# A four-layer graph network: layer 0 by stationary weights, layer 1 begun in layer 0's end, layer 2's tables between layer 1's last lists

## The chip, the cores and the metric

The kernel runs on one core of a Trainium2 chip. The metric is device time in microseconds (us) of one execution. A core has a matrix engine (TensorE, PE in the profile, with its weight loads as PEld), a vector engine (VectorE, DVE), a scalar engine with function tables (ScalarE, ACT), a general engine that here also issues all indirect transfers (GpSimd, POOL), and SyncE (SP), which issues direct transfers. SBUF is the on-chip memory, PSUM holds TensorE's sums.

## The reference

Input x has 8 batches of 2048 nodes with 64 features; adj is a 2048 × 2048 graph of some 8 edges a node, its own edge included. Four layers follow each other; each is `x = layernorm(x + layer(x))`:

```python
# layer 0: graph attention with scores s1(i) + s2(j)
h = layernorm(matmul(x * node_weights + x, W))
e = leaky_relu(h @ a1 [i] + h @ a2 [j], 0.2)
out = elu(softmax(where(adj, e, -big)) @ h + h)
# layer 1: a softmax over the neighbours for each feature
feat = softplus(x * w0 / sqrt(2) + b0)
attn = softmax(where(adj, feat * wa + ba, -big), over neighbours)
out = sum over neighbours of attn * feat
# layer 2: mean over the neighbours, two products, relu twice, layernorm
out = layernorm(relu(x @ W_self + mean(x[neighbours]) @ W_neigh + biases))
# layer 3: attention with scores <h_i, h_j>, four heads, then an output head of the same kind, layernorm
```

## The kernel before, in words

All of x stays in SBUF as `X`, 16 tiles of 128 nodes (NT = 16), each node with 8 × 64 values. A layer that sums over neighbours does so in one of two ways.

*By list.* A tile's neighbours are found by ten indirect gathers (`gather`, L203–204, on POOL): each brings 128 rows of a table in DRAM. There are five slots (GS = 5) for each of two groups of 64 nodes (NG = 2). They are used in three steps per tile, `TOGETHER = ((0, 3), (1, 4), (2,))`, so with 4, 4 and 2 gathers; the code calls a step a quad. A selection matrix `Sel` (0 or 1, fp8) in blocks of 32 nodes adds the gathered rows into their nodes by a matmul.

*By matrix.* For the tiles 0 to DENSE − 1 the adjacency itself stands in SBUF as `ET` in fp8. A block of 128 × 128 is multiplied with the rows of a whole tile, and these rows are split into three bf16 pieces (high, middle, low), whose three matmuls add up to f32.

The stages, in the order of time:

1. The adjacency is read, lists, `Sel` and `ET` are made; the table of layer 0 (`htab0`, 512 values a row) is written.
2. **Layer 0** (L432–524), all 16 tiles by list, in an order written by hand (`manual_schedule`). In each round of the loop: `fetch` gathers the next tile's ten blocks into `hs` (two buffers of a whole tile); `weights` forms the scores and two exponentials; `divide` and `combine` end an earlier tile; `weigh` multiplies every gathered row by its weight on DVE (L476, five products of 128 × 1024) and adds the products up with `self_`, the selection in f32, as stationary operand (L482), and the denominators with 12 small matmuls (L484); `activate` does the ELU and, every second tile, the layer norm's statistics; `normalise` applies them on ACT (L170, eight activations a tile). The score of the neighbour, a2·h, stands in the place of the first feature of a row; `combine` gets that feature back as minus the sum of the others (L498), since h is centred.
3. **Layer 1's rows** (`make_rows`, L570–597), four tiles at once, in an order left to the scheduler: exp and log on ACT (softplus), logits on DVE, exp on ACT, a product on DVE (L590), a write to the table `rtab`; then the pieces into `R`: high on POOL (L593), rest on DVE (L595), middle on ACT (L596), low on POOL (L597). TensorE adds the first three dense tiles' matmuls behind (L605).
4. **Layer 1's sums.** `finish` divides (L614) and adds to X, and where both tiles of a pair are done, normalises them. The dense tiles 3 to 7 run in steps of one block, and between them the quads of tiles 15 down to 8 (L660); gathers go two quads ahead into 8 buffers.
5. **Layer 2's tables** (L812–824). For every tile: X turned by TensorE, two products into `py` (two buffers), `y` copied and written to `ytab` by SyncE, `Y`'s pieces by POOL (high, L818), DVE (rest, L822), ACT (middle, L823), POOL (low, L824), and `S` by DVE (L819). Again the scheduler sets the order.
6. **Layer 2's sums**, by hand: dense steps (L982), quads (L962), and in their gaps each tile's chain of normalisations. `show` copies a finished tile on POOL into `Xo` and writes it to layer 3's table `xtab` (L908–912).
7. **Layer 3**, by hand, with two further lists of 160 gathers each.

In stages 2, 4, 6 and 7 POOL issues gathers in program order; a gather waits until its buffer is free, and what stands behind it on POOL waits too. SyncE's queue works in order as well.

Of the kernel before, what the change touches and what calls it, by code (L numbers as in the profile page):

```python
# [48 lines left out]
def kernel(ctx: ExitStack, tc: tile.TileContext, ins: dict, out: bass.AP):  # L49
# [150 lines left out]
    DENSE = 8  # L200
# [23 lines left out]
    htab0 = dram.tile([N + 1, BD], F32, name="htab0")  # L224
    no_row(htab0)
    l0 = ExitStack()
    wp = l0.enter_context(tc.tile_pool(name="l0w", bufs=1))
    H = wp.tile([P, NT, BD], F32, name="H")
# [33 lines left out]
    for k, a in enumerate((a1, a2)):  # L262
# [5 lines left out]
        if k:  # L268
            first_col = wp.tile([P, 2], F32, name="first_col")
            nc.vector.tensor_copy(first_col, Wv[:, :, 0])  # L270
            nc.vector.tensor_copy(Wv[:, :, 0], Wa[:, 1])
            nc.vector.tensor_copy(Wa[:, 1], first_col)

# [13 lines left out]
    def node_products(t0, wk, ps):  # L287
# [4 lines left out]
        for q in range(HALF):  # L292
# [14 lines left out]
            nc.vector.tensor_reduce(var[:, q], sq[:, :, 1:], AX.X, ALU.add)  # L307
            held.append(ph)
        v4, r4, t4 = (a.rearrange("p q (a k) -> p q a k", k=2) for a in (var, rstd, tmp))
        nc.vector.tensor_tensor(t4, pq[:, :, :, 1], pq[:, :, :, 1], ALU.mult)  # L310
        nc.vector.tensor_tensor(var, var, tmp, ALU.add)
        nc.vector.scalar_tensor_tensor(var, var, 1.0 / D, eps.unsqueeze(2).to_broadcast(var.shape), op0=ALU.mult, op1=ALU.add)
        inv_sqrt(*(a.rearrange("p q b -> p (q b)") for a in (rstd, var, tmp)))
        for q, ph in enumerate(held):
            t = t0 + q
            nc.vector.tensor_tensor(H[:, t].rearrange("p (b d) -> p b d", d=D),
                                    ph.rearrange("p a (k d) -> p (a k) d", d=D), along(rstd[:, q]), ALU.mult)
            nc.sync.dma_start(htab0[t * P:(t + 1) * P, :], H[:, t])
# [116 lines left out]
    wk = l0.enter_context(tc.tile_pool(name="l0k", bufs=2))  # L435
    ps_e = l0.enter_context(tc.tile_pool(name="l0pse", bufs=2, space=PSUM))
    ps_o = l0.enter_context(tc.tile_pool(name="l0pso", bufs=3, space=PSUM))
    ps_w = l0.enter_context(tc.tile_pool(name="l0psw", bufs=1, space=PSUM))
    held, zs, stats = {}, {}, {}

    def fetch(it):
        hs = wk.tile([P, GS * NG, B, D], F32, name="hs")
        for s in range(GS):
            for g in range(NG):
                gather(hs[:, s * NG + g].rearrange("p b d -> p (b d)"), htab0, it, s, g)
        selTf = wk.tile([P, GE], F32, name="selTf")
        nc.scalar.activation(selTf, SelT[:, it], AF.Copy)
        self_ = wk.tile([P, NG, NQ, GB], F32, name="self_")
        nc.scalar.activation(self_, Sel[:, it], AF.Copy)
# [3 lines left out]
        pe = ps_e.tile([P, GS, NG * B], F32, name="pe")  # L453
        for s in range(GS):
            nc.tensor.matmul(pe[:, s], selTf[:, s * P:(s + 1) * P], s1g.rearrange("p g b -> p (g b)"), start=True, stop=True)
        held[it] = hs, self_, pe

    def weights(it):
        hs, self_, pe = held[it]
        wm = wk.tile([P, GS * NG, B], F32, name="wm")  # L460
        nc.vector.tensor_tensor(wm, pe.rearrange("p s (g b) -> p (s g) b", b=B), hs[:, :, :, 0], ALU.add)
        w = ps_w.tile([P, GS * NG, B], F32, name="w")
        nc.vector.scalar_tensor_tensor(w, wm, 0.2, wm, op0=ALU.mult, op1=ALU.max)
        nc.scalar.activation(wm, w, AF.Exp)
        nc.scalar.activation(w, w, AF.Exp)  # L465
        held[it] = hs, self_, w, wm

    def weigh(it):
        hs, self_, w, wm = held[it]
        po = ps_o.tile([P, BD], F32, name="po")  # L470
        pd = ps_w.tile([P, B], F32, name="pd")
        for n, ss in enumerate(TOGETHER):
            for s in ss:
# [11 lines left out]
        held[it] = po, pd  # L485

    def divide(it):
        po, pd = held.pop(it)
        rd = wk.tile([P, B], F32, name="rd")
        nc.vector.reciprocal(rd, pd)  # L490
        z = zs[it] = po.rearrange("p (b d) -> p b d", d=D)
# [1637 lines left out]
```

## Time and profile before

| | us |
|---|---|
| three runs: median (lowest to highest) | 1773.65 (1766.21 to 1776.88) |
| profiled execution: its time, its span | 1766.28, 1764.5 |
| adjacency, tables of layer 0 | 0 to 184 |
| layer 0, gathers | 184 to 397 |
| layer 0, end | 397 to 445 |
| layer 1, rows | 445 to 529 |
| layer 1, sums | 529 to 684 |
| layer 2, tables | 684 to 748 |
| layer 2, sums | 748 to 924 |
| layer 3 | 924 to 1764 |

Over the span TensorE is busy 1388.2 us (79%), DVE 1197.8 (68%), ACT 931.5 (53%), POOL 870.1 (49%). The bounds of the stages are those between the first and last instructions of a kind, rounded. A line of groups reads: line, engine, operation, target and sources, their shapes, how often; busy time and mean ns of one; idle time of the engine before them, and what ended most of it. A line of the timeline begins with the start and the duration in us, and the idle time before it stands in brackets.

### The profile page before, as it was taken

What the parts mean: (1) busy time and instruction counts of PE and PEld (TensorE: products, weight loads), DVE (VectorE), ACT (ScalarE), POOL (GpSimd) and SP (SyncE); (2) the same over time, 40 slices, a digit from 0 to 9 for tenths busy, and PEclk for the clock granted to TensorE, in tenths of its full rate; (3) what the DMA queues carried; (4) which work ended last, traced back from release to release, by engine and by line L of the source; (5) the groups of instructions that cost most, each with busy time, mean ns of one, the idle gap of its engine ahead of it and who ended that gap; (6) DMA issues with size and microseconds to landing.
All of it is one profiled execution on the core that took longest, in us unless ns stands there. A gap on an engine that the chain in (4) does not pass through costs nothing.

```text
span 1764.5 us, 38665 instructions
## 1 busy us (share of the span) xinstructions
PE 1388.2 (79%) x15230; PEld 953.8 (54%) x15264; DVE 1197.8 (68%) x2931; ACT 931.5 (53%) x1943; POOL 870.1 (49%) x820
## 2 busy tenths in 40 slices
PE   4673454651689996898839999999999986999994
PEld 3673232330233333632217877777777774878783
DVE  5989389996666564755764666666666654787787
ACT  5763244555942132534654655656655543577674
POOL 0000677670665551766526455454554515777761
PEclk9655567666799998999968999999999998999997
DMA  6550566660227982256614555555555526787771
GB/s 185 182 173 26 174 196 199 190 200 10 95 96 242 332 313 86 90 169 189 174 43 126 144 144 149 150 148 138 150 153 143 144 77 205 206 233 219 212 214 45
DMA packets 154135, 280.64 MB, mean 159 GB/s; under 512 B 64892, under 2 KB 91452, under 8 KB 151868
## 3 DMA queue, kind: packets, MB, share of 16 engines
q0 software_dynamic: 56320, 189.44, 35.8%
q1 hardware_dynamic: 80986, 84.45, 16.5%
q10 hardware_dynamic: 16640, 4.20, 1.1%
q8 instruction: 123, 2.02, 0.5%
q14 instruction: 66, 0.54, 0.1%
HBM read 237.60 MB, written 40.42 MB: 158 GB/s over the span
## 4 chain that ended last, share of the span: by engine, by line
PE 42%; DVE 13%; ACT 6%; issue 5%; POOL 3%; DMA 1%; DVEq 0%; SPq 0%; ACTq 0%; POOLq 0%
PE pscore L1081 8%; PE pa L605 6%; PE po L1103 5%; PE pt L1068 4%; PE pscore L1044 4%; PE pa L660 2%; PE ps L1385 2%; PE po L1424 2%; PE py L812 2%; DVE z L1156 2%; POOL hs L204 1%; PE pt L1362 1%; PE pa L982 1%; ACT z L849 1%; PE pscore L1166 1%
## 5 line engine op out<-in xcount | busy, mean ns | idle before, releaser
L204 POOL DMA_INDIRECT hs<-htab,src x160 | 153.2, 958 | 238.6 <-issue 221.5
L204 POOL DMA_INDIRECT xs<-xtab,src x160 | 205.9, 1287 | 115.6 <-PE po L1103 63.3
L1087 DVE SCALAR_TENSOR_TENSOR w<-w,Sel 128x640 f32<-128x640 f32 (+2 forms) x160 | 153.2, 958 | 135.3 <-ACT w L1084 134.6
L605 PE MATMUL pa<-R,ET 128*128 128x512 bf16 x746 | 178.3, 393 | 52.0 <-POOL R L593 35.3
L204 POOL DMA_INDIRECT hs<-ktab,src x160 | 158.7, 992 | 63.6 <-issue 35.7
L1081 PE MATMUL pscore<-U,xsT 64*128 64x80 f32 (+2 forms) x2560 | 183.0, 283 | 0.0
L1081 PEld LDWEIGHTS pscore<-U,xsT 64*128 64x128 f32 x2560 | 157.7, 190 | 43.5 <-ACT xsT L1070 22.7
L605 PEld LDWEIGHTS <-ET 128*128 128x128 fp8e4 x768 | 75.2, 100 | 163.6 <-issue 84.4
L170 ACT ACTIVATE X<-X,ln_m,ln_r 128x64 f32<-128x64 f32 x256 | 87.2, 427 | 138.7 <-DVE ln_m L162 138.7
L1070 ACT COPY xsT<-pt 128x512 f32<-128x512 f32 x160 | 93.6, 585 | 104.1 <-PE pt L1068 104.1
L1084 ACT ACTIVATE w<-pscore 128x640 f32<-128x640 f32 (+2 forms) x160 | 119.5, 747 | 47.1 <-PE pscore L1081 45.2
L1103 PE MATMUL po<-w,xs 128*64 128x88 f32 (+2 forms) x3072 | 139.0, 236 | 0.7 <-DVE w L1087 0.7
L1068 PE MATMUL pt<-ident,xs 128*128 128x128 f32 x640 | 106.8, 290 | 23.5 <-DMA xs<-xtab,src 22.8
L1103 PEld LDWEIGHTS po<-w,xs 128*64 128x64 f32 x3072 | 113.4, 137 | 14.9 <-DVE w L1087 0.8
L204 POOL DMA_INDIRECT rs<-rtab,src x80 | 75.9, 949 | 62.4 <-PE pa L660 42.6
L614 DVE RECIPROCAL rec<-pa 128x256 f32<-128x256 f32 x32 | 54.1, 1729 | 64.0 <-PE pa L660 38.0
L1385 PE MATMUL ps<-U,hsT 128*128 128x64 f32 x768 | 93.8, 269 | 1.5 <-ACT hsT L1363 1.5
L476 DVE TENSOR_TENSOR hs<-hs,w 128x1024 f32<-128x1024 f32 x80 | 91.8, 1213 | 2.7 <-ACT w L465 2.6
L1385 PEld LDWEIGHTS ps<-U,hsT 128*128 128x128 f32 x768 | 92.5, 192 | 1.9 <-ACT hsT L1363 1.7
L982 PE MATMUL pa<-Y,ET 128*128 128x512 bf16 x372 | 89.1, 386 | 3.1 <-DVE rest L822 2.1
L1472 ACT ACTIVATE z<-z,ln_m,ln_r 128x64 f32<-128x64 f32 x240 | 83.5, 431 | 14.1 <-DVE ln_m L1460 14.1
L204 POOL DMA_INDIRECT rs<-ytab,src x80 | 76.8, 960 | 26.8 <-issue 17.0
(636 smaller groups left out, 3059.8 us busy)
## 6 DMA issues: line engine op xcount, KB each, us to landing
at<-in_adj SPq DMA_DIRECT2D x16, 1024.0 KB
R<-itab SPq DMA_DIRECT2D x60, 256.0 KB
rtab<-r SPq DMA_DIRECT2D x16, 512.0 KB
ptab<-hp SPq DMA_DIRECT2D x16, 384.0 KB
hi<-ptab SPq DMA_DIRECT2D x16, 384.0 KB
ktab<-hb SPq DMA_DIRECT2D x16, 260.0 KB
X<-in_x ACTq DMA_DIRECT2D x16, 256.0 KB
htab<-H SPq DMA_DIRECT2D x16, 256.0 KB
```

Source lines behind the costliest of these rows:

```text
L170: nc.scalar.activation(v[:, b], v[:, b], AF.Identity, scale=rstd[:, k:k + 1], bias=nmr[:, k:k + 1])
L204: nc.gpsimd.indirect_dma_start(out=dst, out_offset=None, in_=table[:, :], in_offset=bass.IndirectOffsetOnAxis(ap=src[:, it, s, g:g + 1], a ...
L476: nc.vector.tensor_tensor(wx, wx, along(w[:, own].rearrange("p g b -> p (g b)")), ALU.mult)
L605: nc.tensor.matmul(po[h].rearrange("p a f -> p (a f)"), ET[:, jt, it * P:(it + 1) * P], R[:, jt, q, h].rearrange("p a f -> p (a f)"), star ...
L982: nc.tensor.matmul(sums[it], ET[:, jt, it * P:(it + 1) * P], Y[:, jt, q].rearrange("p a n -> p (a n)"), start=(jt == 0 and q == 0), stop=( ...
L1068: nc.tensor.transpose(pt[:, p], xss[k][:, p * P:(p + 1) * P], ident)
L1070: nc.scalar.copy(xsTs[k], pt)
L1081: nc.tensor.matmul(pscore[:, k_, f0:f0 + HN * ni].rearrange("p (h i) -> p h i", i=ni), xsT[half, p], Us[it][half, p, :, i0:i0 + ni], start ...
L1084: nc.scalar.activation(w.rearrange("p k a h i -> p k (a h i)"), pscore[:, :, 0:NP * HN * ni], AF.Exp)
L1087: nc.vector.scalar_tensor_tensor(wt, wt, 3.0e38, edge, op0=ALU.min, op1=ALU.mult)
L1103: nc.tensor.matmul(po[half, p, :, a - blk * GB:b - blk * GB], xs[:, f0:f0 + D], w[:, k_, p, :, a - WINDOWS[s][0]:b - WINDOWS[s][0]], start ...
L1385: nc.tensor.matmul(pscore[:, g, 2 * p:2 * p + 2], hsT[:, g, p], U[:, p, :, node_block(g, k)], start=False, stop=(p == NP - 1))
```

## The change

DENSE becomes 7, so that tile 7 too goes by list in layers 1 and 2: 9 tiles, 27 quads, 90 gathers in each of the two.

Layer 0: a row of `htab0` gets 66 values a batch: the score, a one, and the 64 features. The weights are multiplied into the selection (`W`, four DVE products a tile), and `W` is the stationary operand against the gathered rows (32 columns against 65 values, 96 matmuls a tile); the column of ones gives the denominator. `hs` is held in half tiles with five buffers.

Layer 1's rows move into layer 0's loop: `normalise` also does the exp, `soften` the log every second round, then `logits` and `row_out`, which writes `rtab`. What is left of layer 0's end and of the rows is written out by hand. The pieces are no longer made from the row in SBUF: `load_rows` reads it back from `rtab` on SyncE into `rf` (two buffers), and `pieces` splits it, for tiles 0 to 4 (SOON = 5) on POOL alone, in the end of layer 0, for the others on ACT and DVE between the matmuls. Tile 0's first five blocks are multiplied in the end of layer 0.

Layer 1's sums run in an order by hand: 18 of the 27 quads (AMID) between the dense steps, six gathers in flight (8 buffers before), a finished tile's statistics and scaling some steps later (`later`, `due`). Layer 2's tables (`turn_x`, `products`) are made between the last nine quads, with `py` in one buffer. Buffers in these parts are waited for tile by tile (`reuse_waits="tile"`), and `S` and `Y` are one tile for each of the 16. The code of layer 2's sums and of layer 3 changes in names only.

The core of the diff:

```diff
-    DENSE = 8
+    DENSE = 7
...
     def fetch(it):
-        hs = wk.tile([P, GS * NG, B, D], F32, name="hs")
...
+        hs = [wk.tile([P, GS, B, E0], F32, name="hs", bufs=5) for _ in range(NG)]
...
     def weigh(it):
-                nc.vector.tensor_tensor(wx, wx, along(w[:, own].rearrange("p g b -> p (g b)")), ALU.mult)
...
+                nc.vector.tensor_tensor(W[:, of[0]:of[-1] + 1], Sel[:, it, g, of[0]:of[-1] + 1].unsqueeze(2).to_broadcast(shape),
+                                        pe[:, 1, g, ss[0]:ss[-1] + 1].unsqueeze(3).to_broadcast(shape), ALU.mult)
+            for n in range(NQ // 2):
+                for t in range(B):
+                    j, b = divmod(t, HB)
+                    for q in (n, n + NQ // 2):
+                        s, k = QS[q]
+                        nc.tensor.matmul(pv[node_block(g, k), j, b], W[:, q, t], hs[g][:, s, t, 1:], start=(n == 0 and b == 0),
+                                         stop=(n == NQ // 2 - 1 and b == HB - 1))
...
+            if k >= 3:
+                normalise(k - 3)
+                if k % 2 == 0:
+                    soften(k - 4)
+            if k % 2 and k >= 5:
+                logits(k - 5)
+                logits(k - 4)
+            if k % 2 == 0 and k >= 6:
+                row_out(k - 6)
+                row_out(k - 5)
...
+    def load_rows(jt):
+        if jt < NT:
+            rfs[jt] = ra.tile([P, 2 * BD], F32, name="rf", bufs=2)
+            nc.sync.dma_start(rfs[jt], rtab[jt * P:(jt + 1) * P, :])
+
+    def pieces(jt):
+        if jt < NT:
+            rf = rfs.pop(jt)
+            hi, mid, lo = (R[jt][:, q].rearrange("p h a n -> p (h a n)") for q in range(3))
+            if jt < SOON:
+                nc.gpsimd.tensor_copy(hi, rf)
+                nc.gpsimd.tensor_tensor(rf, rf, hi, ALU.subtract)
+                nc.gpsimd.tensor_copy(mid, rf)
+                nc.gpsimd.tensor_tensor(lo, rf, mid, ALU.subtract)
+                return
+            nc.scalar.copy(hi, rf)
+            nc.vector.tensor_tensor(rf, rf, hi, ALU.subtract)
+            nc.scalar.copy(mid, rf)
+            nc.vector.tensor_tensor(lo, rf, mid, ALU.subtract)
...
+        load_rows(0)
+        load_rows(1)
+        row_out(NT - 6)
+        row_out(NT - 5)
+        for t in range(SOON):
+            pieces(t)
+            load_rows(t + 2)
+            add_rows(0, t)
+        combine(NT - 2)
+        divide(NT - 1)
+        activate(NT - 2)
+        normalise(NT - 3)
+        soften(NT - 4)
+        combine(NT - 1)
+        activate(NT - 1)
+        logits(NT - 4)
+        logits(NT - 3)
+        normalise(NT - 2)
+        normalise(NT - 1)
+        row_out(NT - 4)
+        row_out(NT - 3)
+        soften(NT - 2)
+        for t in (NT - 2, NT - 1):
+            logits(t)
+        for t in (NT - 2, NT - 1):
+            row_out(t)
...
+    AMID, LATE = 18, 14
+    n = 0
+    with tc.manual_schedule(engines=engines):
+        fetch(IN_FLIGHT)
+        pieces(SOON)
+        load_rows(SOON + 2)
...
+        for k, (it, jt) in enumerate(steps):
+            if made < NT and (k % 3 == 2 or jt + 2 >= made):
+                pieces(made)
+                load_rows(made + 2)
+                made += 1
+            add_rows(it, jt)
+            if jt == NT - 1:
+                finish(it)
+            due()
+            if k >= LATE and n < AMID and (k - LATE) * AMID >= n * (len(steps) - LATE):
+                add_edges(n)
+                n += 1
...
+    with tc.manual_schedule(engines=engines):
+        shown, count = [], 0
+        while count < NT:
+            if n < len(quads):
+                add_edges(n)
+                n += 1
+            due()
+            due()
+            if n == len(quads) and not normal and len(shown) == count:
+                while later and not normal:
+                    due()
+            for _ in range(1 if n % 2 else 2):
+                if normal:
+                    t = normal.pop(0)
+                    turn_x(t)
+                    shown.append(t)
+                if count < len(shown) - 1 or (count < len(shown) and not normal):
+                    products(shown[count])
+                    count += 1
```

## The prediction

> **What bounds the kernel now.** I read the table of busy time by stage first, because the mean shares (TensorE 79%) mix stages with different limits. Columns: window and its length, then busy us (instructions) of PE, weight load, DVE, ACT, POOL, then granted clock, DMA share, GB/s.
>
> ```profile
> 184.00:397.00 213.00, 112.20 (x853) 66.98 (x855) 168.82 (x330) 92.22 (x281) 153.24 (x160) 0.68 0.68 196
> 397.00:445.00 48.00, 7.28 (x71) 3.61 (x66) 29.84 (x80) 28.68 (x71) 1.46 (x2) 0.61 0.05 15
> 445.00:529.00 84.00, 69.27 (x268) 28.83 (x274) 57.16 (x44) 60.12 (x68) 55.19 (x31) 0.88 0.24 97
> 529.00:684.00 155.00, 152.63 (x864) 56.59 (x877) 92.19 (x230) 36.54 (x104) 76.72 (x86) 1.00 0.76 272
> 684.00:748.00 64.00, 42.37 (x202) 34.71 (x204) 41.72 (x87) 36.92 (x80) 31.94 (x41) 0.87 0.21 74
> 748.00:924.00 176.00, 131.95 (x623) 47.47 (x632) 112.26 (x415) 89.86 (x244) 92.15 (x104) 0.87 0.51 144
> ```
>
> Row by row: layer 0's gathers (DVE and POOL near full, TensorE at 0.68 of its clock); layer 0's end, in which nothing is half busy but DVE and ACT, so a chain of waits; layer 1's rows; its sums, bound by TensorE (152.6 of 155); layer 2's tables; layer 2. The stretches before 184 (DVE) and after 924 (layer 3, 840 us) the diff leaves almost alone. Next the groups of instructions:
>
> ```profile
> L204 POOL DMA_INDIRECT hs<-htab,src x160 | 153.2, 958 | 238.6 <-issue 221.5
> L476 DVE TENSOR_TENSOR hs<-hs,w 128x1024 f32<-128x1024 f32 x80 | 91.8, 1213 | 2.7 <-ACT w L465 2.6
> L605 PE MATMUL pa<-R,ET 128*128 128x512 bf16 x746 | 178.3, 393 | 52.0 <-POOL R L593 35.3
> L204 POOL DMA_INDIRECT rs<-ytab,src x80 | 76.8, 960 | 26.8 <-issue 17.0
> ```
>
> A gather costs POOL 0.96 and, back to back, 0.30 of issue: 1.26. So 20 gathers, a pair of tiles, cannot take under 25.2; in the middle of the loop the pair takes 27.1.
>
> **Layer 0's loop.** Removed per tile: five products of 1.213 (L476), 6.07, and the sum over the row (L498, 0.69). Added: four DVE multiplies of 128x768. The trace has no such op on selection and PSUM weights; layer 3's are near:
>
> ```profile
> L1087 DVE SCALAR_TENSOR_TENSOR w<-w,Sel 128x768 f32<-128x768 f32 x32 | 30.7, 960 | 63.2 <-ACT w L1084 63.2
> L1397 DVE TENSOR_TENSOR w<-Sel,w_mid 128x512 f32<-128x512 fp8e4 x16 | 11.1, 691 | 8.0 <-ACT w_mid L1375 8.0
> L1424 PE MATMUL po<-hs,w 128*32 128x65 f32 x2048 | 73.5, 226 | 6.2 <-DVE w L1397 6.2
> ```
>
> About 0.9 each, 3.6 a tile. So DVE falls by some 3 of 12.3 us. TensorE's 12 matmuls of 512 values (and 12 of 8) become 96 of 32 columns by 65 values, each recorded as two instructions. In layer 3 thirty-two such instructions in the same alternation take 1.05 us by the timeline: 96 matmuls are 6.3 us at full clock; at half clock the issue of 54 ns an instruction gives 10.4. I take 8, since this stage's clock was 0.68, and keep both ends.
>
> The new chain within a pair goes through ACT, which now also does exp, Ln (two table loads of 1.28 a pair) and row exponentials. After the odd tile: W 3.6 + activate 1.3 + statistics 4.2, all DVE, then ACT's normalise 2.76, f 0.74, two row exponentials 1.15, selection copy 0.62, softmax exp: 14.75 to the next W. After the even tile ACT gives 11.35, or TensorE plus the divide 8 + 4.4 = 12.4. Pair: 26.1 to 27.2 against 27.1; at 10.4 it is 14.75 + 14.8, 29.3 with overlap. I take −3 for the loop, range −10 to +20. The adjacency stage loses a few 16-element ops, −2.
>
> **Layer 1's start.** Before, 132 us lie between the last layer-0 gather (397) and layer 1's first gather (529.8): the end chain 48, rows 84. After, rows of twelve tiles are written inside the loop, so only the last four and their norms follow. From the last W at about 398, the written order gives matmuls, divide, combine, activate, statistics (4.2), two norms split between DVE and ACT, Ln with table load, logits, last row product: about 50 us, to 446–452. SyncE then still holds these two row writes behind the reload for tile 7, which waits for DVE's pieces of tile 5: gathers begin near 457. POOL makes the pieces of tiles 0 to 4 alone, 2 × 1.04 to 1.44 and 2 × 2.12 each, 32 to 38 us, ending about 445–450; there TensorE's steps begin. POOL beside DVE has a price in the trace:
>
> ```profile
> 516.78 1.44 POOL L593 CAST R<-r 128x1024 bf16<-128x1024 f32 x1 [1.75 <-DVE r L590]
> 518.18 2.12 POOL L597 TENSOR_TENSOR R<-rest,R 128x1024 bf16<-128x1024 f32 x1
> 518.24 3.13 DVE L595 TENSOR_TENSOR rest<-r,R 128x1024 f32<-128x1024 f32 x1 [0.93 <-POOL R L593]
> ```
>
> DVE's 1024-wide subtraction takes 1.23 elsewhere (at 469.96) and 3.13 beside POOL's. The Trainium skill ("SBUF — State Buffer", section "Who interferes with whom") gives a reason: the engines share a port pair under an exclusive lock. By that rule every two-input DVE op of the tail could wait for one of POOL's ten subtractions, an estimate of up to 10 × 1.9 = 19 us on the chain; by the row alone, where one in several met, I count 4, in the 50.
>
> **Layer 1's sums.** DENSE 7 leaves 7 × 16 × 6 = 672 matmuls at 0.2155 (pitch at clock 1.00), of which 30 are done in the tail: 642 × 0.2155 = 138.4. Eighteen of the 27 list steps stand here: 18 × 1.93 = 34.7 (mean L660 work per step). With 3% of gaps, 178: from 450 to about 628. Before, all dense and all 24 list steps end at 684: −56.
>
> **Layer 2's tables.** Before, 64 us for 16 tables (5.44 a pair in the steady part). After, nine list steps are mixed in, and POOL's order is fixed: the gathers of a step, then per table the cast, a wait, and the last subtraction.
>
> ```profile
> 742.80 0.61 POOL L818 CAST Y<-y 128x512 bf16<-128x512 f32 x1
> 743.45 0.69 DVE L822 TENSOR_TENSOR rest<-py,Y 128x512 f32<-128x512 f32 x1
> 744.36 0.62 ACT L823 CAST Y<-rest 128x512 bf16<-128x512 f32 x1
> 745.10 1.15 POOL L824 TENSOR_TENSOR Y<-rest,Y 128x512 bf16<-128x512 f32 x1
> ```
>
> From the cast's end (743.41) to the subtraction (745.10) POOL waits 1.7. Before, the next table's cast at 744.53 lay in that hole; in the new order nothing can. So up to the last list step, with 24 gathers left and 13 tables: 24 × 1.26 = 30, 13 × (0.61 + 1.15 + 0.2) = 26, 13 × 1.7 = 22: 78, ending at 706 (up to 82). Behind it tile 7's finish 5.1, statistics 4, norm 5.4 and the tables of 9, 6 and 7 in turn, with POOL's memsets, about 32. Layer 2's first gather: 738 to 744, I take 741, against 748.0. Thus the stage grows from 64 to 113 and eats 49 of the 56. If half of the tables can run ahead, the low end is 85.
>
> **Layer 2.** POOL issues 80 gathers from 748.0 to 877.85; after, 90: ten more, 12.6. It waits 26.8 in all, some of which shrinks with 48 fewer dense matmuls (10 us of TensorE): I take +9, range +3 to +14. Layer 3's code is unchanged.
>
> **Sum** against the profiled execution (1766.3; span 1764.5): 741 − 748 = −7, + 9 = +2, so 1768. The median shown is 7.4 above that execution; by it the sum would be 1776. I forecast 1770. A measurement of this kernel can tell about 1% from no change.
>
> **Rivals.**
> - *Tables hide between the lists.* For it: TensorE is busy only 42 of 64 there and POOL 32. Against: POOL's fixed order. At 85 instead of 113: 1768 − 28 = 1740. With a loop at its floor too (−7 more): 1733.
> - *Slower: TensorE stays at half clock in layer 0.* The window shows 0.68 and after it 0.61. It decides from 8.2 us a tile up, where TensorE plus the divide passes the ACT branch that closes the pair. At 10.4, 7.5 pairs × 2.7 = +20: 1788. The Trainium skill ("TensorE: Matmul & The Clock Gate", section "What's actually happening") has a half clock after an idle window of about 3.4 us and a full one after a busy one; by that the denser TensorE would warm up, an estimate of 6.3 a tile and a loop bound by ACT. No run here shows it yet.
> - *The rows aren't ready.* The row writes or reloads come late on SyncE, or POOL's pieces hold the tail: the change then doesn't start layer 1 early. If steps begin at 475 rather than 450: 1768 + 25 = 1793.
>
> **Chances.** Forecast (within 1% of 1773.65, so 1756 to 1791) 0.43; tables hidden, faster, 0.31; half clock 0.12 and rows late 0.14, both counted slower: the first lies at the bound, and the sum by the median would put it 8 higher. The range goes from the first rival's better time, 1733, to a little past the last's, 1796, and leaves some 2 in 10 outside.
>
> **What would show it.** Right: a layer-0 pair at 26–27 us, first gather of the row table near 457, layer 1's dense matmuls ended near 628, POOL waiting for ACT's middle piece 1.7 us a table, layer 2's first gather near 741 and its last near 880. Wrong: a DVE multiply far from 0.9, TensorE waiting on pieces after 460, a table stage of under 95 us, or a changed time in layer 3, where the diff has nothing.

## The result, and the profile after

The changed kernel takes 1791.44 us (1790.56 to 1792.95, four runs), the kernel before 1772.94 us (1766.21 to 1776.88, four runs): ratio 1.0114, 95% interval 1.0091 to 1.0137. It is 1.1% slower, a small difference but clear of the noise, as the interval lies above 1. The forecast was 1770, no change; the measured time lies inside the range that the prediction gave, near its upper end.

The profiled execution took 1792.95 us (span 1791.2) against 1766.28 (span 1764.5). The points in time at which a stage begins or ends are read from the first and last start of an instruction (a tile's instructions list both); the forecast's points are those of the prediction's steps:

| point, us from the span's start | before | forecast | after |
|---|---|---|---|
| first gather of layer 0 | 184.1 | 182 | 187.4 |
| last gather of layer 0 | 395.5 | 390.5 | 389.8 |
| first gather of layer 1 | 529.8 | 457 | 465.7 |
| last dense matmul of layer 1 | 683.3 | 628 | 637.7 |
| last list matmul of layer 1 | 676.5 | 706 | 727.7 |
| first gather of layer 2 | 748.0 | 741 | 766.2 |
| first gather of layer 3 | 924.2 | 926 | 946.1 |
| end | 1764.5 | 1766.5 | 1791.2 |

The busy time by stage of the kernel after, in the same columns as before (window and its length, busy us and instructions of PE, weight load, DVE, ACT, POOL, then granted clock, DMA share, GB/s):

```profile
187.00:390.00 203.00, 130.96 (x2838) 126.37 (x2838) 136.90 (x332) 112.65 (x280) 154.14 (x160) 0.74 0.79 233
390.00:466.00 76.00, 48.55 (x503) 28.01 (x504) 56.69 (x97) 41.02 (x78) 34.01 (x22) 0.79 0.35 120
466.00:639.00 173.00, 164.65 (x859) 61.59 (x860) 102.27 (x199) 48.46 (x106) 67.64 (x67) 0.97 0.67 225
639.00:766.00 127.00, 78.26 (x349) 44.07 (x341) 62.00 (x140) 43.33 (x96) 52.37 (x67) 0.81 0.41 137
766.00:946.00 180.00, 138.37 (x602) 44.25 (x600) 113.65 (x412) 90.46 (x245) 101.68 (x115) 0.89 0.54 155
946.00:1791.00 845.00, 777.48 (x11710) 627.85 (x11710) 545.87 (x1004) 481.57 (x909) 455.05 (x386) 0.95 0.57 157
```

Layer 0 is now bound by POOL's gathers (154 of 203 us busy, and 0.3 of issue for each of the 160 fills nearly all of the rest). The stretch from there to layer 1's first gather is down from 133 to 76 us. Row four, the tables with the last nine list steps, eats it: 127 us in which no engine is busy for even two thirds; before, the tables had 64. The groups that answer to those shown of before:

```profile
L204 POOL DMA_INDIRECT hs<-htab,src x160 | 154.9, 968 | 231.1 <-PE pe L466 182.9
L628 PE MATMUL pa<-R,ET 128*128 128x512 bf16 x672 | 156.4, 389 | 22.3 <-POOL R L610 8.4
L494 PE MATMUL po<-hs,W 128*32 128x65 f32 x3072 | 121.0, 258 | 45.7 <-DVE W L487 22.9
L204 POOL DMA_INDIRECT rs<-ytab,src x90 | 86.5, 961 | 28.4 <-issue 17.4
```

Layer 0's end first. The timeline of the kernel after (start, duration, engine and line, target and sources) at the last layer norm's statistics, beside POOL's pieces:

```profile
433.38 2.12 POOL L611 TENSOR_TENSOR R<-rf,R 128x1024 bf16<-128x1024 f32 x1
433.43 2.10 DVE L142 SCALAR_TENSOR_TENSOR ln_r<-ln_v,guess 128x16 int32<-128x16 int32 x1
435.44 1.04 POOL L608 CAST R<-rf 128x1024 bf16<-128x1024 f32 x1
435.56 0.95 DVE L145 TENSOR_TENSOR ln_t<-ln_r 128x16 f32<-128x16 f32 x1
436.55 0.17 DVE L146 SCALAR_TENSOR_TENSOR ln_t<-ln_t,ln_v 128x16 f32<-128x16 f32 x1
436.56 2.15 POOL L609 TENSOR_TENSOR rf<-rf,R 128x1024 f32<-128x1024 f32 x1
436.75 1.99 DVE L147 SCALAR_TENSOR_TENSOR ln_r<-ln_t,ln_r 128x16 f32<-128x16 f32 x1
```

A DVE instruction on 16 elements a partition, 0.17 us by itself, lasts until POOL's instruction ends: 433.43 + 2.10 = 435.53 against 433.38 + 2.12 = 435.50. It is the same beside POOL's cast (435.56 + 0.95 against 435.44 + 1.04). The statistics (L156 to L162) ran from 431.5 to 445.3, 13.8 us; the prediction had 4.2 for them.

Then the table stage: the waits between 639 and 766 (who waited for what: us in total, times, longest), and one table's round in the timeline:

```profile
DVE S L800 <- ACT y L797: 51.6, 13, 8.3
ACT Y L804 <- DVE rest L803: 49.7, 16, 8.7
POOL Y L805 <- ACT Y L804: 36.2, 16, 7.5
PE py L793 <- DVE rest L803: 35.6, 9, 9.1
```

```profile
724.45 1.97 PE L793 MATMUL py<-Wsn,xT 128*128 128x256 f32 x8 [2.05 <-DVE rest L803]
726.49 0.59 ACT L797 COPY y<-py 128x512 f32<-128x512 f32 x1 [1.05 <-POOL Y L805]
727.14 0.61 POOL L799 CAST Y<-y 128x512 bf16<-128x512 f32 x1 [0.95 <-ACT y L797]
727.78 0.69 DVE L803 TENSOR_TENSOR rest<-py,Y 128x512 f32<-128x512 f32 x1
728.51 0.62 ACT L804 CAST Y<-rest 128x512 bf16<-128x512 f32 x1 [1.43 <-DVE rest L803]
728.69 1.68 PE L793 MATMUL py<-Wsn,xT 128*128 128x256 f32 x7
```

Four engines (TensorE, ACT, POOL, DVE) wait for each other in a ring: the product fills `py`, ACT copies it to `y`, POOL casts `y`, DVE takes the rest from `py` and the cast. The next table's product (728.69) can start only when the rest (727.78) has been read out of the one `py` buffer, 4.24 us after the product ahead. POOL's waits for the middle piece (36.2 us in all), which the prediction counted, are no link of this round.

### The profile page after: what moved, and what is told of

It is laid out like the page before. It is cut to its first block, busy times and chain, and to the rows that moved or that the text cites. A ratio compares the mean times of both kernels' runs of the same rounds, so it can differ in the third digit from the quotient of the medians.

```text
span 1791.2 us, 43134 instructions
## 1 busy us (share of the span) xinstructions
PE 1442.7 (81%) x17480; PEld 1026.4 (57%) x17480; DVE 1166.5 (65%) x2919; ACT 919.2 (51%) x1897; POOL 869.2 (49%) x829
## 5 line engine op out<-in xcount | busy, mean ns | idle before, releaser
L204 POOL DMA_INDIRECT hs<-htab,src x160 | 154.9, 968 | 231.1 <-PE pe L466 182.9
L628 PE MATMUL pa<-R,ET 128*128 128x512 bf16 x672 | 156.4, 389 | 22.3 <-POOL R L610 8.4
L494 PE MATMUL po<-hs,W 128*32 128x65 f32 x3072 | 121.0, 258 | 45.7 <-DVE W L487 22.9
L204 POOL DMA_INDIRECT rs<-rtab,src x90 | 90.6, 1006 | 132.1 <-PE pa L728 95.5
L170 ACT ACTIVATE X<-X,ln_m,ln_r 128x64 f32<-128x64 f32 x240 | 81.8, 428 | 127.7 <-DVE ln_m L162 127.7
L494 PEld LDWEIGHTS po<-hs,W 128*32 128x32 f32 x3072 | 116.9, 136 | 48.5 <-DVE W L487 24.9
L628 PEld LDWEIGHTS <-ET 128*128 128x128 fp8e4 x672 | 65.2, 99 | 119.4 <-issue 48.2
L204 POOL DMA_INDIRECT rs<-ytab,src x90 | 86.5, 961 | 28.4 <-issue 17.4
L1165 PEld LDWEIGHTS pt<-ident,xs 128*128 128x128 f32 x640 | 68.3, 143 | 38.2 <-issue 23.1
```

Of the source, the lines that this page charges most:

```text
L170: nc.scalar.activation(v[:, b], v[:, b], AF.Identity, scale=rstd[:, k:k + 1], bias=nmr[:, k:k + 1])
L204: nc.gpsimd.indirect_dma_start(out=dst, out_offset=None, in_=table[:, :], in_offset=bass.IndirectOffsetOnAxis(ap=src[:, it, s, g:g + 1], a ...
L494: nc.tensor.matmul(pv[node_block(g, k), j, b], W[:, q, t], hs[g][:, s, t, 1:], start=(n == 0 and b == 0), stop=(n == NQ // 2 - 1 and b == ...
L628: nc.tensor.matmul(po[h].rearrange("p a f -> p (a f)"), ET[:, jt, it * P:(it + 1) * P], R[jt][:, q, h].rearrange("p a f -> p (a f)"), star ...
L1165: nc.tensor.transpose(pt[:, p], xss[k][:, p * P:(p + 1) * P], ident)
```

## The experiments

All of them ran on other chips than the first measurement. There the kernel before takes 1872.8 to 1885.6 us (group medians and its profiled run), so times are compared within that set only: with the kernel before's own profile (label p_before) and the kernel after's (c1_after). Stages in us, from the same starts as above; "end" is from layer 0's last gather to layer 1's first, "to dense" from there to layer 1's last dense matmul, "to tables" from that to layer 2's first gather:

| run | layer 0's gathers | end | to dense | to tables | layer 2 | span |
|---|---|---|---|---|---|---|
| before, first chip | 211.4 | 134.3 | 153.5 | 64.7 | 176.2 | 1764.5 |
| after, first chip | 202.4 | 75.9 | 172.0 | 128.5 | 179.9 | 1791.2 |
| p_before | 232.6 | 134.4 | 154.1 | 64.1 | 182.2 | 1871.0 |
| c1_after | 275.1 | 81.1 | 171.0 | 130.3 | 201.1 | 1962.1 |
| e1_rest_from_y | 277.1 | 80.2 | 170.7 | 119.7 | 199.4 | 1948.2 |
| e2_finish_late | 276.6 | 80.4 | 171.1 | 129.1 | 201.9 | 1956.3 |
| t1_lo_dve | 277.0 | 80.1 | 171.7 | 122.6 | 199.3 | 1954.2 |
| t3_lo_dve_y | 277.0 | 81.0 | 170.8 | 115.9 | 201.0 | 1958.2 |
| t4_lists_first | 275.6 | 78.9 | 208.4 | 86.0 | 201.4 | 1947.8 |
| e3_tables_after | 276.5 | 80.1 | 206.7 | 62.3 | 199.0 | 1920.6 |
| f1_skewed_tail | 275.0 | 83.3 | 212.4 | 68.9 | 197.6 | 1941.5 |
| e4_no_pool_pieces | 275.4 | 66.6 | 169.6 | 132.8 | 199.6 | 1951.1 |
| e6_tail_pieces | 276.7 | 82.8 | 174.5 | 128.8 | 198.1 | 1966.1 |
| b1_layer0_only | 276.6 | 141.3 | 154.9 | 64.9 | 182.6 | 1916.1 |
| b3_quarter | 229.1 | 133.0 | 153.6 | 64.5 | 182.1 | 1862.3 |
| b2_dense7 | 238.2 | 134.3 | 176.9 | 73.4 | 200.9 | 1920.4 |
| v1_after_d8 | 269.2 | 79.7 | 216.2 | 65.8 | 181.6 | 1924.3 |
| v3_old_l0_seven | 235.4 | 74.7 | 208.4 | 64.6 | 182.3 | 1861.2 |

Each row is one profiled execution. The three stages in the middle agree between the chips to some 5 us (p_before with before, c1_after with after), so what is found of them is taken to hold for the first chip too. The four runs that leave the table stage as it was have 128.5 to 132.8 for it, so a difference of 4 us there says nothing. Layer 0, layer 2 and layer 3's end differ, and are judged here only against p_before.

### The kernel after, again

No edit.

> The kernel after, unchanged, so that the other runs of this group have it on their own chip. On the chip of the prediction it took 1.011 of before. If TensorE's matmuls in layer 0 stand waiting for their own issue here too, as on the chip of the first four runs (73 to 95 us of it in the layer-0 matmuls, none of any size in after's first trace), the ratio is 1.03 to 1.05 and layer 0's gathers take some 277 us; if not, 1.011 and 202.

Measured: 1965.06 us, 1.0479 of before (1.0439 to 1.0519), and 275 us for layer 0's gathers: the case with the slow issue. "Issue" in a profile is idle time for which it shows no releaser. The waits of the first chip and of this one, for the new layer 0's matmuls over the whole span:

```profile
PE po L494 <- issue: 17.3, 7, 5.8
```

```profile
PE po L494 <- issue: 90.6, 115, 16.5
```

Seven waits became 115. Not all of them are what the name says: the seven on the first chip stand at the start of a tile, where `W` (L487) has just come from DVE, and so does the one of 16.5 us here, where the first chip's profile has a wait of 16.44 for `W`. Inside a tile the first chip has none, and this run 113 with 73.0 us. The granted clock in layer 0's gathers is lower too, 0.67 against 0.74, with TensorE 170 us busy instead of 130; whether it is lower because TensorE stops so often, or part of the cause, was not separated. In the timeline of e1_rest_from_y it looks like this:

```profile
335.24 0.33 PE L494 MATMUL po<-hs,W 128*32 128x65 f32 x4 [0.39 <-issue]
336.68 0.40 PE L494 MATMUL po<-hs,W 128*32 128x65 f32 x5 [1.12 <-issue]
338.14 0.44 PE L494 MATMUL po<-hs,W 128*32 128x65 f32 x4 [1.06 <-issue]
```

### Layer 0's new form alone

The kernel before with layer 0's wide rows, `W` and half-tile buffers; all else as before, DENSE 8.

> The kernel before with layer 0's new form alone (wide rows, stationary weights, half-tile buffers); rows of layer 1, sums and tables as before, DENSE 8. By the trace of after the gathers take 202 instead of 213 us, and start 3 later: -7 to -10 in all, 1757 on the scale of 1766. By the prediction's terms (loop -3, adjacency -2): 1761. Rival: the rows in the loop are what moved it, or the end of layer 0 grows as the gathers shrink (ACT still has the divides and norms): 1766 or more.

Measured: 1925.36 us, 1.0271 of before (1.0251 to 1.0292). All of it is layer 0: 276.6 us of gathers against 232.6, and 7 more in its end. Here layer 0's form is a loss of 45 us, far above both expectations, where on the first chip the same loop, with the rows in it, was 9 us shorter. The loss here is in the loop without the rows in it.

### The same data through a quarter of the instructions

```diff
-                for t in range(B):
-                    j, b = divmod(t, HB)
+                for j in range(2):
                     for q in (n, n + NQ // 2):
...
-                        nc.tensor.matmul(pv[node_block(g, k), j, b], W[:, q, t], hs[g][:, s, t, 1:], start=(n == 0 and b == 0),
+                        nc.tensor.matmul(pv[node_block(g, k), j], W[:, q, j * HB], hs[g][:, s, j * HB:(j + 1) * HB, 1:], start=(n == 0),
```

> The kernel before with the new layer 0, and one edit: four batches go through one matmul (24 a tile of 260 columns instead of 96 of 65), all with the weights of the first of the four, so the other batches' own weights are left out; the same rows are gathered and streamed. Theory of issue: layer 0's gathers fall from 277 to 203 to 212, the total from 1916 to about 1850. Rival (the streaming or the gathers themselves are slow on this chip): 260 or more, 1900.

Measured: 1864.17 us (1916.1 to 1862.3 in span), layer 0's gathers 229.1. Same gathers, same columns streamed, a quarter of the matmuls and weight loads (the other three batches' own weights are left out): 47.5 us gone. The waits for issue inside a tile fell by about as much, from 74.8 us in 117 stops in b1_layer0_only to 23.7 in 25. So the loss goes with the number of TensorE's instructions; matmuls and weight loads were not separated. The stage did not come down to the 203 to 212 expected, and neither does before's:

### Before, on these chips

No edit.

> The kernel before, unchanged, for its profile on the chip of this group (it took 1874 to 1876 on the two chips of the earlier groups, 1766 to 1777 on the first). Theory of issue: TensorE's instructions arrive too slowly there for the new layer 0 (192 multiplications and 192 weight loads a tile), not for the old one (24 and 24): layer 0's gathers take 211 to 220, the waits for issue sit in layer 3's second part (363 instead of 296 us) and nowhere else. Rival (transfers or the matrix clock are slower there): layer 0's gathers take 250 or more here too. Layer 2 (first gather to layer 3's first) at 183, as with the new layer 0 alone: then DENSE 7 costs 18 there, not 4.

Measured: 1872.84 us. Layer 0's gathers take 232.6, more than the 211 to 220 of the theory and less than the rival's 250. The old layer 0 too is some 20 us longer here than on the first chip, with 24 matmuls a tile; the waits for issue at its small matmuls (`pd`, L484) grew by 12:

```profile
PEld pd L484 <- issue: 43.8, 114, 1.3
```

against

```profile
PEld pd L484 <- issue: 32.0, 87, 0.7
```

on the first chip, each from 190 us to the end of its gathers (418 and 397). Whether these 12 us are part of the 20, and what the rest is, stays open. The granted clock, 0.69 on both chips, is not it. Layer 2 takes 182, so the 198 to 202 of the runs with DENSE 7 are 15 to 20 more.

### The end of layer 0 without POOL's pieces

```diff
-                nc.gpsimd.tensor_copy(hi, rf)
-                nc.gpsimd.tensor_tensor(rf, rf, hi, ALU.subtract)
-                nc.gpsimd.tensor_copy(mid, rf)
-                nc.gpsimd.tensor_tensor(lo, rf, mid, ALU.subtract)
+                for piece in (hi, mid, lo):
+                    nc.gpsimd.memset(piece, 1.0)
```

> The kernel after without POOL's splitting of tiles 0 to 4: their three pieces are set to a constant by memsets (which read no SBUF), so this part of layer 1's sum is left out. Theory of the shared port: DVE's statistics of tiles 14 and 15, 13.8 us from 431.5 beside POOL's subtractions, fall to 4.2, layer 1's first gather comes some 12 us earlier (466 -> 454), the total falls by as much, 1779. Theory that ACT's chain and SyncE's queue set the end (table loads, last row writes behind the reload of tile 7): the statistics shorten, but the first gather stays within 3 us of 466, 1788 or more.

The split of tiles 0 to 4 is left out, their pieces are a constant. Measured: 1953.15 us. From layer 0's last gather to layer 1's first 66.6 instead of 81.1; the span 11 shorter than c1_after's. The statistics take 6.2 us with two other subtractions (1.21 and 1.22) among them; the small ones are back at 0.17:

```profile
509.05 1.65 DVE L156 BATCH_NORM_STATS2 st<-X 128x6 f32<-128x128 f32 x8
510.62 1.21 DVE L612 TENSOR_TENSOR rf<-rf,R 128x1024 f32<-128x1024 f32 x1
511.74 0.17 DVE L159 SCALAR_TENSOR_TENSOR ln_v<-st,eps 128x16 f32<-128x16 f32 x1
511.95 0.18 DVE L142 SCALAR_TENSOR_TENSOR ln_r<-ln_v,guess 128x16 int32<-128x16 int32 x1
512.16 0.17 DVE L145 TENSOR_TENSOR ln_t<-ln_r 128x16 f32<-128x16 f32 x1
```

So POOL's pieces cost the chain 14.5 us. Against c1_after's timeline, 13.0 of them are DVE instructions that became shorter: the statistics 7.6 (13.8 to 6.2), two products (L556) 2.8, eight scalings (L540) 1.8, two further products (L551) 0.8. This run's memsets stand beside the statistics before these (from 487.9 on), and the small instructions there kept 0.17 and 0.18. The Trainium skill ("SBUF — State Buffer", section "Who interferes with whom") has a port pair that GpSimd and VectorE share under an exclusive lock; by it a VectorE instruction with two SBUF inputs contends with a GpSimd instruction that reads SBUF, and not with one that only writes it. The rows agree: casts (1.04) and subtractions (2.12) held DVE, memsets did not.

### The same pieces on ACT and DVE

The five tiles' casts and subtractions are issued one step at a time between `combine`, `activate`, `normalise` and so on; POOL makes none.

> The kernel after, one edit: the pieces of tiles 0 to 4 are made by ACT and DVE in steps between the parts of layer 0's end, POOL makes none. Leaving POOL's pieces out shortened the end by 13.6 us (80.2 to 66.6 from the last layer-0 gather to layer 1's first, on one chip). DVE now has 10 subtractions of 1.23, ACT 10 casts of 1.04. If they fit into the idle time of the two engines: end 68 to 72, total -6 to -10. If they stand in the chain: 12 longer than without POOL, so 78 to 80 and no gain.

Measured: 1967.94 us, the end 82.8 (81.1 in c1_after): no gain, the second case. Ten subtractions of 1.23 on DVE are as much as the lock took. The chain through DVE has no room for the pieces, whether DVE makes them or waits for POOL to read.

### The table stage: the buffer

```diff
-        nc.vector.tensor_tensor(rest, py[:, :, 1], hi, ALU.subtract)
+        nc.vector.tensor_tensor(rest, y, hi, ALU.subtract)
```

> The kernel after, one edit: a table's rest is taken from y in SBUF instead of from py, so that the one py buffer is free once y and S are read, without POOL's cast between. Theory of the one buffer: a table's round trip (product 1.97, y 0.58, cast 0.61, rest 0.69 and four hand-overs, 4.2 us) falls to some 3.5, so about 13 tables x 0.7 = 9 us off the table stage (639 to 766), 1782. Theory of the prediction (POOL's fixed order with its 1.46 to 1.7 us holes is the bound): POOL's order and holes stay, so the stage stays within 2 us, 1791. Theory that DVE's order is the bound (finish and statistics, 10 us, in front of a table's S and rest): no more than 4 us, since the long waits stay.

Measured: 1950.01 us; the stage falls from 130.3 to 119.7, -10.6 against the -9 of the theory of the one buffer, the 2 at most of the prediction's, and the 4 at most of DVE's order.

### The table stage: DVE's order

`finish` of a list tile is put behind the round's tables (`put_off` holds the tile, two lines).

> The kernel after, one edit: in the table stage the finish of a list tile (reciprocals, products, sums: 5.1 us of DVE, and the statistics that follow) is issued behind the tables of its round, not ahead. Theory that DVE's order bounds the stage: the waits of 6.9, 7.1 and 7.5 us of POOL for a middle piece shrink to 1.5, -12 of the 128 us stage. Theory of the one py buffer: under -4, since each table still takes its round trip of 4.2. Theory of the prediction (POOL's holes): 0.

Measured: 1958.44 us; the stage 129.1, -1.2. That theory falls: POOL's longest wait for a middle piece went from 7.5 to 5.8 and not to 1.5, and DVE's for `y` from 8.2 to 10.3.

### The table stage: POOL's order

```diff
-        nc.gpsimd.tensor_tensor(lo, rest, mid, ALU.subtract)
+        late.append((lo, rest, mid))
...
         nc.gpsimd.tensor_copy(hi, y)
+        last_piece()
```

with `last_piece` the same subtraction on DVE.

> The kernel after, one edit: a table's last piece (1.15 us on POOL, behind the 1.46 us wait) is made by DVE, one table later. Theory of the prediction (POOL's order with its holes bounds the stage): 13 x (1.46 + 1.15 + 0.2) = 36 us less of POOL's time up to the last list step, stage 130 -> 95 to 105. Theory of the one buffer's round trip: POOL's last piece is not part of it, DVE takes 0.69 more where it waits anyway: 126 to 133.

Measured: 1956.00 us; the stage 122.6, -7.7. Neither theory: POOL's last piece is worth something, but a fifth of the 36 that the prediction's sum gave it. With both edits:

> Both edits: last piece by DVE, rest taken from y so that py is free early. Theory of the one buffer: as the run with the second edit alone (119.7) within 4. If POOL's holes bind once the buffer is free early: 90 to 110.

Measured: 1959.99 us, the stage 115.9. Together they give -14.4, less than their sum (-18.3). This is just within the 4 of 119.7 that the one buffer's theory allowed, and not the 90 to 110 of POOL's holes. The span gained nothing from it: 3.9 lower than c1_after's, with 7 more in layer 3's first part.

### The table stage: lists and buffer apart

All 27 list steps between the dense matmuls (AMID 27); the table loop with its order and its one buffer stays.

> The kernel after with all 27 list steps between the dense matmuls, and its own table loop unchanged (order by hand, one py buffer). Theory of the one buffer: 16 round trips of 4.2 to 4.7 and the head make 75 to 85 from the last list step to layer 2's first gather, against 62 with two buffers and the scheduler's order. If the list steps between the tables are what stretches the stage, and not the buffer: 60 to 68. From layer 1's first gather to layer 2's first: 207 + that.

Measured: 1949.60 us. Without any list in it the loop still takes 86.0 from the dense end (88.9 from the last list step, above the one buffer's 75 to 85 and far from the 60 to 68 of the other theory), and TensorE waits as before for the rest:

```profile
PE py L796 <- DVE rest L806: 32.3, 15, 7.5
```

And the tables behind the lists with two `py` buffers, in the scheduler's order, as before the change:

```diff
-    AMID, LATE = 18, 14
+    AMID, LATE = 27, 14
...
-    pa = turned.enter_context(tc.tile_pool(name="l2py", bufs=1, space=PSUM, reuse_waits="tile"))
+    pa = turned.enter_context(tc.tile_pool(name="l2py", bufs=2, space=PSUM, reuse_waits="tile"))
...
+    for t in normal:
+        turn_x(t)
+        products(t)
```

> The kernel after with its last part undone: all 27 list steps between the dense matmuls, then the 16 tables by themselves in the scheduler's order with two py buffers, as before the change. Theory that mixing costs: nine list steps more add 9 x 1.93 = 17.4 to the dense stage (ends 639 -> 656), the tables take the 64 us they took before, layer 2's first gather at 720 instead of 766, total -46, 1745. Rival (the mixing hides work, and the stage is long for the lists' own sake, their gathers and finishes): the first gather stays at 755 to 775, 1781 to 1800. In between: the last norms are not hidden, 735, 1760.

Measured: 1933.06 us, 1.0334 of before (1.0286 to 1.0382); 62.3 for the tables. From layer 1's first gather to layer 2's: c1_after 301.3, t4_lists_first 294.4, e3_tables_after 269.0. Taking the lists out, by itself, is worth 7; the second buffer and the scheduler's order together then 25. The expected -46 was too much, since the dense stage grew by 36 and not by 17.4: a list step there costs 4 us, not 1.93. TensorE waits for gathers (six in flight) in the run with all lists there:

```profile
PEld pa L728 <- DMA rs<-rtab,src: 29.8, 16, 4.7
PE pa L728 <- DMA rs<-rtab,src: 15.2, 10, 4.2
```

An order by hand with two buffers, in which a table's cast stands ahead of the last piece of the table before, and the pieces of tiles 0 to 4 on ACT and DVE:

> The kernel after with the tables behind all lists, two py buffers and an order by hand in which a table's cast comes before the last piece of the table ahead of it, so that POOL's hole is filled; and the pieces of tiles 0 to 4 on ACT and DVE. From the last list step to layer 2's first gather 62 with the scheduler's order; 16 tables at 2.7 (before's pace) and a head of 8 make 51. With dense and lists at 207 from layer 1's first gather (as measured with all lists there) that is 258 instead of 300, and -6 from the end: total -48 against after on the same chip, so 0.985 of before where after is 1.011. If the lists between the dense matmuls wait for their gathers longer than measured, or the skew gains nothing: -25, 0.997.

Measured: 1946.16 us, 1.0386 of before (1.0352 to 1.0420); the tables 68.9 (71.8 from the last list step, where 51 was expected). Filling POOL's hole by hand was worse than the scheduler's order (62.3). With one buffer the order by hand took 86.0, so of e3_tables_after's gain the buffer has more than the order, as far as two different orders by hand can be compared.

### DENSE 7

The kernel before with `DENSE = 7`.

> The kernel before with DENSE 7 alone. Layer 2 went from 182 to 200 on these chips wherever DENSE was 7, whatever else was changed: here too 198 to 202. Layer 1's first gather to dense end: 96 matmuls less (some of them before the first gather) and three list steps more, 154 to 140 to 160. Total +10 to +25 against 1871. Rival (the 200 comes from the buffers that wait tile by tile): 183 to 188.

Measured: 1922.21 us, the span 49.4 above p_before's, where +10 to +25 was expected: layer 2 +18.7, layer 1's sums +22.8 (expected -14 to +6), tables +9.3, layer 0 +5.6, the rest -7. The rival (buffers that wait tile by tile) falls, as this kernel has none. In layer 2 TensorE's wait for gathers grows; p_before first, then b2_dense7:

```profile
PEld pa L962 <- DMA rs<-ytab,src: 31.1, 19, 5.7
```

```profile
PEld pa L962 <- DMA rs<-ytab,src: 47.0, 35, 7.2
```

One more list tile costs layer 2 more here than the 14 us that the prediction allowed as the most; on the first chip it was 3.7, in the whole change. Alone, layer 0's form (+45.1) and DENSE 7 (+49.4) each cost about half of what the whole change costs on these chips (+91.1). What either costs alone on the first chip was not measured.

The kernel after with DENSE 8 and the tables behind the lists (and `wm` in one buffer):

> The kernel after with the tables behind all lists (as in the run of that name, 1921 us of span) and DENSE 8: 96 more matmuls in layer 1 (+20.7), three list steps less (-5.8 and their waits for gathers), layer 2 with 80 gathers instead of 90 (201 to 183). Sum about -8 to -15: 1908, 1.018 of before. Rival (layer 2's 201 is not DENSE's doing): 1925 or more.

Measured: 1926.28 us, 1.0244 of before (1.0187 to 1.0301). Layer 2 fell to 181.6 as expected; but the sums of layer 1 took 216.2 instead of 206.7, and the span was that of e3_tables_after, 1924.3 against 1920.6. The total is thus near the rival's 1925, but layer 2's fall speaks against the rival itself. Starting layer 1 early leaves its dense matmuls to do: when layer 1's first gather is issued, before has done 288 of 768 dense matmuls (three tiles' sums run behind the rows), the kernel after, by the first chip's timeline, some 112 of 672 (this run 114 of 768).

### Old layer 0, rows in its loop, tables behind the lists

Before's `fetch`, `weights`, `weigh`, `divide` and `combine`; after's rows in the loop and layer 1 by hand with seven gathers in flight; two `py` buffers; DENSE 8.

> Before's layer 0 (products on DVE, few matmuls), layer 1's rows in its loop, layer 1 in its hand-written order with seven gathers in flight instead of six, tables behind all lists, DENSE 8. On a chip where issue is slow the loop falls from 277 to 215 to 225 (rows' work fills DVE), the rest as in the run with DENSE 8: about 1908 - 55 = 1853, 0.99 of before. If the rows lengthen the old loop (DVE had 12.3 of 13.5 us busy) to 245: 1.00 to 1.005. On the first chip: 0.99 to 1.00.

Measured: 1868.82 us (ten runs) against 1875.84 (thirteen), 0.9963 of before (0.9933 to 0.9992): the one version below both kernels, by 0.4% of before, where 0.99 was expected. It was not run on the first chip. The old loop holds the rows at 235.4 (232.6 without), the first gather of layer 1 comes 58 us earlier than in p_before (494.0 to 552.4), and layer 1's sums give 54 of it back (208.4 against 154.1).

## Why the prediction was right or wrong

By the first chip's two profiles, step by step, as changes against before: forecast, then measured.

| step | forecast | measured |
|---|---|---|
| up to layer 0's first gather | -2 | +3.3 |
| layer 0's gathers | -3 | -9.0 |
| layer 0's end and layer 1's rows | -68 | -58.4 |
| layer 1's first gather to dense end | +17.5 | +18.5 |
| from there to layer 2's first gather | +48 | +63.8 |
| layer 2 | +9 | +3.7 |
| layer 3 | 0 | +4.8 |
| sum | +2 | +26.7 |

**Right.** Layer 0's pair of tiles came down to POOL's floor (202.4 us for eight pairs); a multiply of 128x768 took 0.89 (3.54 for four) against the 0.9 set, and the matmuls of a tile 6.8 to 8.8 us by the timeline against 8. The balance was right in kind: layer 1 begins 64 us earlier, and the table stage gives that back, but all of it and not 48. The rival of a half clock didn't come for the stage (0.74 in that window, and the loop 9 us shorter), though the matmuls of a tile looked at began at half clock (0.50 from 375 to 381 us, 0.92 from there to 383); nor did the one of hidden tables. The rival of late rows came in part: POOL's pieces did hold the tail, and the first gather was 9 us late, not 25.

**Right by luck, the dense stage.** It was met within 1 us, but of two errors. Some 112 of the 672 matmuls were done before the first gather, and the forecast's own steps leave room for about 62 by then: 50 at 0.2155, 11 us less to do. Against that, 560 × 0.2155 + 18 × 1.93 = 155 us of work took 172, 17 us of gaps where 3% (5 us) were allowed.

**Wrong, the table stage, +15.5.** This is the step that failed. It said that POOL's fixed order, casts, 1.7 us holes and last pieces, sets the pace. The hole is there (1.46), but the runs give POOL's last piece 7.7 us of the stage and not 36, and the one `py` buffer 10.6; both edits together took 14.4 off, nearly the 15.5. A loop without lists still took 86, against 62 with two buffers and the scheduler's order. Resources were read one by one from POOL's column; the change's line `bufs=1` made a ring through four engines of 4.24 us a table, longer than POOL's own 3.4 (0.61 + 1.46 + 1.15 + 0.2). The diff shows it, and the prediction named the buffer in no term. The loop is not all of the stage's 130 us: the other 44 came with the nine list steps, 4.9 each; moved between the dense matmuls they cost 4 each there, where the forecast had 1.93 for a step.

**Wrong, the end of layer 0, +9.4.** The mechanism was named (POOL's subtraction holds DVE) and mis-sized: 4 us "in the 50", because only the wide subtraction beside it was counted. It measured 14.5 (81.1 to 66.6). Small instructions lose most: a chain of twelve at 0.17 us each took 12.1 instead of 2.5, since seven of the twelve lasted 0.90 to 2.10. The estimate of up to 19 that followed from the Trainium skill's rule on the shared port was the better end of that bracket, though it counted the subtractions alone, and the casts held DVE too.

**Wrong, smaller terms.** Layer 0 gained 6 more than forecast, and its start came 5.3 later: the bounds of layer 1 (six small DVE instructions, L443 to L452, 1.0 us in all) now stand in the adjacency stage's DVE work, and the first products on loaded values start at 9.68 instead of 8.17, behind one more write on SyncE. This was read from the timeline and not tried, and half of the 5.3 stays open. Layer 2's +9 was 5 too much on the first chip and 10 too little on the others. Layer 3's +4.8 lies in code that didn't change, most of it in the stretch between its two lists, where the granted clock was 0.84 and 0.82 against 0.90 twice; the other three runs of the kernel after have spans 1.5 to 2.4 us shorter. Its cause was not tried.

The sign came from two errors in one direction, 15.5 and 9.4, on a balance of +2 in a kernel of 1766. The other five steps missed by up to 6 us each, and that they add up to 0 is luck, as it is that the total stayed inside the range. A forecast of "no change" by two terms of 50 to 70 with opposite signs carries the error of both.

## What to carry to other kernels

When work is moved into the gaps of another stage, follow one item around every engine and buffer that it passes; with one buffer the round trip can be the pace, and no engine's busy time shows it. Don't put POOL's reads of SBUF beside a chain of small VectorE instructions: here instructions of 0.17 us waited out casts of 1.04 and subtractions of 2.12. An early start is worth only what the stage behind it makes of it: of 64 us, 46 reached the end of the dense matmuls, and 32 of those were 96 matmuls (20.7) and six list steps (11.6) taken out of that stage.

## What the runs showed of the hardware

TensorE can stand idle in the middle of a tile with nothing shown that it waits for, and on some chips only. On the other chips the new layer 0 (192 multiplications and 192 weight loads a tile in the profile) had 72 to 95 us of such issue time, in 115 to 134 stops, most of them about 1 us or less; seven of the twelve runs count in it one stop of 16 us ahead of the first tile, which is a wait for `W`, and without it the sum is 69 to 79. On the first chip there were 7 stops, all at the start of a tile. A quarter of the instructions on the same data took 47.5 us off the stage. That TensorE waits there for its instructions to arrive fits this, but was not seen directly, and the granted clock of that stage is lower there as well (0.67 against 0.74). So the same change of layer 0 is -9 us on one chip and +42 on another (both with layer 1's rows in the loop). The profile pages count 140 instruction transfers on the larger of the two instruction queues for the kernel after and 123 for before, on either kind of chip; whether each is slower there, or slower beside the gathers' traffic, was not tried. The code of layer 3's second half, with the same kind of small matmuls, takes 357 to 365 us there and 296 on the first chip, for the kernel before as well (363 and 296), at a granted clock of 0.86 and 0.94.
